# Selective scan: the diagonals of B for one of three pairs of states, made by VectorE in one product per block instead of ScalarE in four activations

## The chip, the cores and the metric

The kernel is written for Trainium2 and runs on one core of one chip. Times are device microseconds (us) of the whole program. Three timed runs gave a median of 30857.69 us (30847.12 to 30858.35). Beside them stands one profiled execution, from which every duration below comes.

## The reference

Four layers follow each other on an image tensor of 4 x 64 x 64 x 192: x = x + layer(group_norm(x)). Layer 0, 1 and 3 are selective scans, Layer 2 is a Toeplitz mixer. The change concerns Layer 3 alone, whose core is:

```python
proj = jnp.einsum('kbcl,kcd->kbld', xs, x_proj_w)          # four ways k of reading the image
Bm, Cm = proj[..., dr:dr + N], proj[..., dr + N:]          # N = 16 states
delta = jax.nn.softplus(...)                               # per position and channel
def step(state, inp):
    d, b, c, uu = inp
    dA = jnp.exp(d[..., None] * A_neg[:, None, :, :])
    state = dA * state + (d * uu)[..., None] * b[:, :, None, :]
    y = jnp.einsum('kbcn,kbn->kbc', state, c)
    return (state, y)
```

There are 192 channels, 16 states and 4096 positions for each of four ways and each of four images. The part that matters here is the input of the recurrence, `(d * uu) * b`: for each state n, the value delta*u of a channel and position times B of that state at that position.

## The kernel before

**Tiling.** Layer 3 takes one image after the other (`ss2d`). For each, `ss2d_input` makes the normalized and convolved u, `ss2d_scan` scans it, `ss2d_output` sums up and projects. A scan is cut into 32 jobs: four ways (two forward, two reversed, in the order forward, reversed, forward, reversed) times eight chunks of 512 positions. A job has three groups of 64 channels. A tile of 128 partitions holds 64 channels twice, for two halves of the states; with two states along the free axis, one tile of 128x1024 holds a group and a pair index p (0 to 3), that is four states. So a job has 12 units (group, p). Their order is written out by hand in `TWO` and `ONE`; in this text they are numbered in that order: unit 0 (p 0), 1 (p 0), 2 (p 3), 3 (p 1), 4 (p 1), 5 (p 3), 6 (p 2), 7 (p 2) for the first two groups, then 8 (p 0), 9 (p 3), 10 (p 1), 11 (p 2) for the third.

**A unit.** `feed` makes `b`, the input of the recurrence, two units ahead (`AHEAD`), and `dA`, two exponentials of ScalarE (line 401). `scan` runs the recurrence on VectorE, two instructions of 128x512 (line 418, `h`), with `dA` in SBUF and `b` in PSUM; then GpSimd multiplies by C (line 422, `hc`, 128x1024). `collect` sums over the states on TensorE (line 447, `y`). A carry copy on ScalarE (line 428) saves the last state for the next chunk.

**How b is made.** For p 0, 1 and 2 TensorE makes `b` out of `dtuT`, which is delta*u with positions on the partitions, times a diagonal matrix that holds B of one state over 128 positions (line 378). These diagonals, `diag`, are made in `fetch`: for each of four blocks of 128 positions (`part`, `NB` = 4) and each of four states one activation on ScalarE, identity times a column of `bt` (line 332). That is 48 activations of 128x128 in a job. For p 3 (`direct`) GpSimd multiplies instead (line 351, `bs`), so GpSimd has 12 `hc` and 3 `bs` in a job.

**Other work of a job.** `project` and `turn_b` make `xd` and `bt`; `step_size` and `finish` make delta (ScalarE, with a softplus and its two table loads) and `dtu` (VectorE, line 278, both inputs in SBUF); `turn` transposes it. At the end of each of two channel parts, `add` writes the result: in forward ways ScalarE copies `y`, in reversed ways VectorE adds the earlier way's result (line 614, `out`). The second part has 64 rows and goes through a fold on TensorE first (`fold_ps`, line 625).

**What sets the order.** `plan` gives each load and each block of a diagonal a step: a diagonal for p is due `LEAD_DIAG` = 10 steps ahead of its first use, one block per step. There are six buffers of `diag`, four of `h`, five of `hc`, three of `dA` and two of `b`. The program is then built by a scheduler that sets the order of instructions on each engine; each engine works through its own order, with waits on the others.

Of the kernel before, what the change touches and what calls it, by code (L numbers as in the profile page):

```python
# [36 lines left out]
class Kernel:  # L37
# [270 lines left out]
    def fetch(self, job, name, key, pools, part):  # L308


        nc = self.nc
        if name in ("both", "dtu2") and job["carry"] is not None:
            one = job[name][key] = pools[name].tile([128, T], F32, name=name)
            of, P, ch = job["delta" if name == "both" else "dtu"], job["P"], key * 64
            while ch < key * 64 + 64:
                t, row = divmod(ch, P)
                rows = min(P - row, key * 64 + 64 - ch)
                for q in range(2):
                    to = q * 64 + ch % 64
                    nc.sync.dma_start(one[to : to + rows, :], of[row : row + rows, t, :])  # L320
                ch += rows
        elif name in ("both", "dtu2"):
            one = job[name][key] = pools[name].tile([128, T], F32, name=name)
            src = job["deltas" if name == "both" else "dtus"][key * 64 : (key + 1) * 64, :]
            for q in range(2):
                nc.sync.dma_start(one[q * 64 : (q + 1) * 64, :], src)
        elif name == "diag":
            if part == 0:
                job["diag"][key] = pools["diag"].tile([128, NB, 4, 128], F32, name="diag")
            for n in range(4):  # L330
                to, of = job["diag"][key][:, part, n, :], job["bt"][:, part, 4 * key + n : 4 * key + n + 1]
                nc.scalar.activation(to, self.ident, AF.Copy, scale=of)  # L332
        else:
            one = pools[name].tile([128, 2 * T], F32, name=name)
            job["cbc" if name == "c" else "bbc"][key] = one
            for q in range(2):
                row = N + 8 * q + 2 * key if name == "c" else 4 * key + 2 * q
                src = job["bc"][row : row + 2, :].rearrange("a l -> (a l)")
                nc.sync.dma_start(one[q * 64 : (q + 1) * 64, :], src.unsqueeze(0).broadcast_to([64, 2 * T]))
# [216 lines left out]
    def ss2d_scan(self, pre, u_d, y_d, P, NT, ways, A, dtb):  # L556
        tc, nc, ins = self.tc, self.nc, self.i
        DI = P * NT
        bufs = dict(c=5, bc=2, diag=5, both=6, dtu2=2) if NT == 3 else dict(c=6, bc=2, diag=6, both=6, dtu2=4)
        with (  # L560
            tc.tile_pool(name="s_w", bufs=2) as pw,
            tc.tile_pool(name="s_prep", bufs=2) as prep,
            tc.tile_pool(name="s_work", bufs=2) as work,
            tc.tile_pool(name="s_c", bufs=bufs["c"]) as cp,
            tc.tile_pool(name="s_bc", bufs=bufs["bc"]) as bcp,
            tc.tile_pool(name="s_diag", bufs=bufs["diag"]) as dp,
            tc.tile_pool(name="s_both", bufs=bufs["both"]) as both,
            tc.tile_pool(name="s_dtu2", bufs=bufs["dtu2"]) as dtu2,
            tc.tile_pool(name="s_mm", bufs=2, space=PSUM) as mm,
            tc.tile_pool(name="s_b", bufs=2, space=PSUM) as bp,  # L570
            tc.tile_pool(name="s_y", bufs=2, space=PSUM) as yp,
        ):
            pools = {"prep": prep, "work": work, "c": cp, "diag": dp, "both": both, "mm": mm, "b": bp, "y": yp,
                     "bc": bcp, "dtu2": dtu2, "bufs": bufs, "behind": 3, "lag": 0}
            jobs = []
            carry = {
                (g, p): pw.tile([128, 2], F32, name=f"carry{g}_{p}", bufs=1)
                for g in range(DI // 64) for p in range(PAIRS)
            }
            when = {  # L580
                3: dict(load=-33, project=-29, turn_b=-27, step_size=(-21, -19, -17), finish=-15,
                        turn=(-12, -10, -8), direct={3: (1,)}),
                2: dict(load=-25, project=-21, turn_b=-19, step_size=(-17, -16), finish=-14,
                        turn=(-9, -8), direct={3: (0, 1)}),
            }[NT]
            direct = when["direct"]

            for k, (col, rev) in sorted(enumerate(ways), key=lambda one: one[1]):
                w = {"dtb": dtb[:, k, :], "A": A[:, k]}

                def weights(k=k, w=w):

                    w["xw"] = self.load(pw, "xw", ins[f"{pre}x_w"][k])
                    w["dtw"] = self.load(pw, "dtw", ins[f"{pre}dt_w"][k])

                for c in range(NCH - 1, -1, -1) if rev else range(NCH):
                    first = not jobs or jobs[-1]["k"] != k
                    job = {"before": {}}
                    s = slice(c * T, (c + 1) * T)

                    def load(job=job, col=col, s=s):
                        job["u"] = self.load(prep, "u", u_d[col][:, :, s])

                    def earlier(t, job=job, col=col, s=s):
                        rows = y_d[col][t * 128 : min(DI, t * 128 + 128), s]
                        job["before"][t] = self.load(work, "earlier", rows)

                    def add(t, job=job, col=col, rev=rev, s=s):
                        y, rows = job["y"][t], min(128, DI - t * 128)

                        def last(y=y):
                            out = work.tile([rows, T], F32, name="out", bufs=3)
                            if rev:
                                nc.vector.tensor_add(out, y, job["before"].pop(t))
                            else:
                                nc.scalar.copy(out, y)
                            nc.scalar.dma_start(y_d[col][t * 128 : t * 128 + rows, s], out)

                        def halves():
                            both = work.tile([128, T], F32, name="out", bufs=3)  # L620
                            nc.scalar.copy(both, y)

                            def sum_them():
                                one = mm.tile([64, T], F32, name="fold_ps", tag="mm")
                                nc.tensor.matmul(one, self.fold, both, start=True, stop=True)
                                return lambda: last(one)

                            return sum_them

                        return halves if rows == 64 else last  # L630

                    steps = [(when["load"], load)]
                    if first:
                        steps.append((when["load"] + (0 if len(jobs) == 0 else -2), weights))
                    if rev:
                        for t in range(-(-DI // 128)):
                            steps.append((8 * t + 2, lambda t=t, earlier=earlier: earlier(t)))
                    job.update(
                        P=P, NT=NT, DI=DI, k=k, w=w, rev=rev, carry=carry, first=first, add=add, y={}, fed={},
                        done={}, bs={}, when=when, steps=steps, direct=direct,  # L640
                    )
                    jobs.append(job)
            self.run_jobs(jobs, pools)
# [586 lines left out]
```

## Time and profile before

| what | value |
|---|---|
| median of three runs | 30857.69 us |
| profiled execution, its own time | 30865.86 us |
| its span | 30864.0 us |
| TensorE, VectorE, ScalarE, GpSimd busy in the span | 26878.4, 22327.6, 23000.6, 22890.6 us |
| activations that make diagonals, all layers | 20480, mean 391 ns |
| of these in Layer 3 | 6144 |
| `hc` in Layer 3 on GpSimd | 1536, median 2367 ns |
| Layer 3's scans | between about 24850 and 30720 us of the span |

The profile lists busy times by engine, groups of instructions with their count, busy time and mean duration, and what ended an engine's idle time. The mean duration of short instructions is longer than the distance at which they follow each other, because records overlap. A record also counts as busy when the instruction stands still behind another engine's use of the same resource. As the layers have different limits, the engine totals of the span say little about Layer 3.

### The profile page before, as it was taken

To read this page: it belongs to the slowest core of one execution; us is meant where nothing else is said; L and a number is where in the kernel's file an instruction comes from. 1 tells how busy PE (TensorE), PEld (TensorE's weight loads), DVE (VectorE), ACT (ScalarE), POOL (GpSimd) and SP (SyncE) were. 2 spreads that over 40 slices of the span, in tenths; PEclk is the share of its full clock that TensorE was granted. 3 is DMA by queue.
4 is the path that set the end of the run, shared out by engine and by line. 5 is a ranking of instruction groups with operands and counts; after the bars stand their busy time and mean duration, and the time that the engine had idled before them with its cause. 6 is when DMAs were issued, how large, how long until landed. Compare 5 with 4: busy or idle time off the path is not lost. (4 is left out here: it accounts for less than half of the span.)

```text
span 30864.0 us, 503255 instructions
## 1 busy us (share of the span) xinstructions
PE 26878.4 (87%) x189464; PEld 15827.7 (51%) x189464; DVE 22327.6 (72%) x16587; ACT 23000.6 (75%) x50177; POOL 22890.6 (74%) x9831
## 2 busy tenths in 40 slices
PE   8998998999899688888888888888588988888888
PEld 5664665666466444444444444444355444444444
DVE  7887888788788777777777777777423267777777
ACT  7885886788588588888888888888232278788888
POOL 7885885888588499989998999999100077777777
PEclk9999999999999899999999999999788999999999
DMA  3334333433433533333333333333533345545454
GB/s 109 100 99 117 101 98 104 112 100 99 119 101 97 142 99 97 97 100 101 101 104 97 98 97 99 102 101 102 131 78 76 104 131 131 132 130 134 128 135 128
DMA packets 1652695, 3342.38 MB, mean 108 GB/s; under 512 B 396725, under 2 KB 453494, under 8 KB 1634646
## 3 DMA queue, kind: packets, MB, share of 16 engines
q1 hardware_dynamic: 1541718, 3142.34, 38.1%
q10 hardware_dynamic: 108544, 167.85, 1.6%
q8 instruction: 1497, 24.53, 0.4%
q14 instruction: 936, 7.67, 0.1%
HBM read 2149.81 MB, written 656.08 MB: 91 GB/s over the span
## 5 line engine op out<-in xcount | busy, mean ns | idle before, releaser
L378 PE MATMUL b<-diag,dtuT 128*64 128x256 f32 x98304 | 12607.9, 386 | 1732.9 <-DVE h L411 917.9
L422 POOL TENSOR_TENSOR hc<-h,c 128x1024 f32<-128x1024 f32 x4608 | 10943.4, 2395 | 1515.0 <-DVE h L418 1158.3
L378 PEld LDWEIGHTS b<-diag,dtuT 128*64 128x64 f32 x98304 | 8214.9, 138 | 6212.3 <-DVE h L411 1903.3
L401 ACT ACTIVATE dA<-both,A 128x512 f32<-128x512 f32 (+1 forms) x12288 | 8267.7, 711 | 2124.3 <-DVE h L411 1472.0
L418 DVE TENSOR_TENSOR_SCAN h<-dA,carry,b 128x512 f32<-128x512 f32 x6720 | 8169.8, 1263 | 1367.8 <-PE b L378 861.4
L422 POOL TENSOR_TENSOR h<-h,c 128x1024 f32<-128x1024 f32 x3072 | 7219.1, 2374 | 1049.2 <-DVE h L411 880.3
L332 ACT ACTIVATE diag<-ident,bt 128x128 f32<-128x128 f32 x20480 | 6570.6, 391 | 92.2 <-issue 91.4
L447 PE MATMUL y<-hc,fold 128*64 128x512 f32 x18432 | 5783.3, 599 | 386.1 <-POOL hc L422 384.4
L411 DVE TENSOR_TENSOR_SCAN h<-dA,b 128x1024 f32<-128x1024 f32 x2304 | 5202.8, 2274 | 1147.3 <-ACT dA L401 798.4
L351 POOL TENSOR_TENSOR bs<-dtu,bc 128x1024 f32<-128x1024 f32 x1536 | 3639.4, 2369 | 158.5 <-DMA c<-bc_dram 72.8
L447 PE MATMUL y<-h,fold 128*64 128x512 f32 x12288 | 3259.6, 593 | 10.2 <-POOL h L422 10.2
L501 POOL MEMSET pad<- 128x13068 f32 (+1 forms) x8 | 73.4, 9172 | 3968.3 <-DMA inw<-in_L_in_w 2997.7
L411 DVE TENSOR_TENSOR_SCAN h<-b,bs 128x1024 f32<-128x1024 f32 x768 | 1758.9, 2290 | 1413.6 <-ACT b L401 1102.8
L447 PEld LDWEIGHTS y<-hc,fold 128*64 128x64 f32 x18432 | 1924.0, 138 | 1550.1 <-POOL hc L422 813.1
L401 ACT ACTIVATE b<-both,A 128x504 f32<-128x504 f32 (+1 forms) x3072 | 2076.2, 676 | 376.4 <-DVE h L418 328.3
L418 DVE TENSOR_TENSOR_SCAN h<-b,carry,bs 128x512 f32<-128x512 f32 x1344 | 1639.2, 1260 | 220.9 <-issue 170.4
L237 PEld LDWEIGHTS dtu_ps<-ident,dtu 128*64 128x64 f32 (+1 forms) x16384 | 1183.2, 141 | 497.6 <-issue 375.9
L447 PEld LDWEIGHTS y<-h,fold 128*64 128x64 f32 x12288 | 1005.0, 137 | 795.2 <-issue 444.9
L418 DVE TENSOR_TENSOR_SCAN h<-dA,b 128x512 f32<-128x512 f32 x960 | 1112.8, 1205 | 352.8 <-PE b L378 191.3
L401 ACT ACT_TABLE_LOAD x1019 | 1307.4, 1283 | 11.8
L237 PE MATMUL dtu_ps<-ident,dtu 128*64 128x128 f32 (+1 forms) x16384 | 1272.7, 273 | 45.9 <-DVE dtu L278 41.5
L827 DVE SCALAR_TENSOR_TENSOR u<-in_ps,conv_w,u 128x504 f32<-128x504 f32 (+2 forms) x1152 | 831.6, 722 | 411.7 <-ACT u L822 402.6
(157 smaller groups left out, 24601.4 us busy)
## 6 DMA issues: line engine op xcount, KB each, us to landing
c<-bc_dram SPq DMA_DIRECT2D x3072, 256.0 KB, 4.1
both<-delta SPq DMA_DIRECT2D x2048, 128.0 KB, 2.7
bc<-bc_dram SPq DMA_DIRECT2D x768, 256.0 KB, 4.2
both<-delta_dram SPq DMA_DIRECT2D x1536, 128.0 KB, 3.7
dtu<-dtu_dram SPq DMA_DIRECT2D x1536, 128.0 KB, 2.7
dtu<-dtu SPq DMA_DIRECT2D x1280, 128.0 KB, 2.5
L_y<-out ACTq DMA_DIRECT2D x512, 256.0 KB, 3.0
u<-L_u SPq DMA_DIRECT2D x160, 768.0 KB, 5.4
```

Of the source, the lines that this page charges most:

```text
L237: nc.tensor.matmul(to[half * 64 : (half + 1) * 64], of[:, half * 64 : (half + 1) * 64], self.ident[:p, :p], start=True, stop=True,)
L332: nc.scalar.activation(to, self.ident, AF.Copy, scale=of)
L351: self.nc.gpsimd.tensor_mul(by(b), dtu, by(job["bbc"][p]))
L378: nc.tensor.matmul(to, dtu, job["diag"][p][:, k, 2 * q : 2 * q + 2, :], start=True, stop=True,)
L401: nc.scalar.activation(to[n], of, AF.Exp, scale=w["A"][:, g, 2 * p + n : 2 * p + n + 1])
L411: nc.vector.tensor_tensor_scan(h[:, way], dA[:, way], b[:, way], 0.0, ALU.mult, ALU.add)
L418: nc.vector.tensor_tensor_scan(hn[:, n, way], dA[:, n, way], by_n[:, n, way], start, ALU.mult, ALU.add)
L422: nc.gpsimd.tensor_mul(hc, h, job["cbc"][p])
L447: nc.tensor.matmul(y[c * 64 : (c + 1) * 64, :], self.fold, of, start=first == 0 and n == 0, stop=last == LAST and n == 1)
L501: nc.gpsimd.memset(pad, 0.0)
L827: nc.vector.scalar_tensor_tensor(u[:, :, to], ps[:, :, of], tap(3 - j), u[:, :, to], ALU.mult, ALU.add)
```

## The change

For p = 2 in Layer 3 the four activations of a block are replaced by one VectorE instruction of 128x512. It multiplies the identity, repeated four times, by four columns of `bt`, each repeated along 128 elements. Layer 0 has an empty list, and Layer 1 has none; their diagonals stay with ScalarE.

```diff
         elif name == "diag":
             if part == 0:
                 job["diag"][key] = pools["diag"].tile([128, NB, 4, 128], F32, name="diag")
+            if key in job.get("whole", ()):
+                by_n = job["bt"][:, part, 4 * key : 4 * key + 4].unsqueeze(2).broadcast_to([128, 4, 128])
+                whole = self.ident.unsqueeze(1).broadcast_to([128, 4, 128])
+                nc.vector.tensor_mul(job["diag"][key][:, part], whole, by_n)
+                return
             for n in range(4):
                 to, of = job["diag"][key][:, part, n, :], job["bt"][:, part, 4 * key + n : 4 * key + n + 1]
                 nc.scalar.activation(to, self.ident, AF.Copy, scale=of)
...
-                        turn=(-12, -10, -8), direct={3: (1,)}),
+                        turn=(-12, -10, -8), direct={3: (1,)}, whole=()),
...
-                        turn=(-9, -8), direct={3: (0, 1)}),
+                        turn=(-9, -8), direct={3: (0, 1)}, whole=(2,)),
...
-                        done={}, bs={}, when=when, steps=steps, direct=direct,
+                        done={}, bs={}, when=when, steps=steps, direct=direct, whole=when["whole"],
```

## The prediction

> **What bounds the kernel now.** I read the page first (engine totals, slices), then looked only at the stretches of Layer 3's scan, because the change touches nothing else. On the page ScalarE and GpSimd are both busy 74 to 75% of the whole span, which decides nothing. The table of windows over single jobs does:
>
> ```profile
> core 0: us, PE busy (x) PEld busy (x) DVE busy (x) ACT busy (x) POOL busy (x), PEclk, DMA share, GB/s
> 28168.70:28208.00 39.30, 34.23 (x255) 20.00 (x253) 30.89 (x25) 37.56 (x96) 35.38 (x16) 1.00 0.53 137
> 28398.30:28435.50 37.20, 33.20 (x262) 20.38 (x260) 31.26 (x27) 36.59 (x95) 36.08 (x16) 1.00 0.56 148
> ```
>
> The first window is one job of a forward way, the second one of a reversed way. The copy that begins a job (`xd<-xd_ps`) recurs every 39.32 us in forward ways and every 37.16 us in reversed ones. ScalarE leaves 1.7 us and 0.6 us of that free: it is the bound. GpSimd is next, with 35.4 to 36.1 us. So a gain can't be larger than the distance to GpSimd. ScalarE's groups over the forward job:
>
> ```profile
> L332 ACT ACTIVATE diag<-ident,bt 128x128 f32<-128x128 f32 x47 | 15.1, 391 | 0.0
> L401 ACT ACTIVATE dA<-both,A 128x512 f32<-128x512 f32 x18 | 11.9, 709 | 1.2 <-issue 1.2
> ```
>
> 15.1 us for 47 is 0.32 us each (the mean of 391 ns overlaps its neighbours). The waits over 28080 to 28640 show how the engines are tied:
>
> ```profile
> PEld y L447 <- POOL hc L422: 78.2, 58, 2.3
> ...
> POOL hc L422 <- DVE h L418: 28.9, 42, 2.4
> ...
> DVE out L614 <- PE y L447: 17.7, 8, 2.5
> ```
>
> Columns: total us, times, longest. TensorE waits for GpSimd, GpSimd for VectorE, and VectorE's `out` for TensorE: a ring in which one late step comes round again.
>
> One VectorE instruction of today has what the new one will have, two inputs in SBUF beside a busy GpSimd: `dtu`. By source line over Layer 3, and in the timeline of a forward job:
>
> ```profile
> L278 DVE TENSOR_TENSOR dtu<-delta,u x128: 1194/1839/3002, 24861.3 to 30642.7; 96x1024 f32<-96x1024 f32 x128
> ```
>
> ```profile
> 28148.55 5.63 POOL L422 TENSOR_TENSOR hc<-h,c 128x1024 f32<-128x1024 f32 x2
> ...
> 28150.11 1.86 DVE L278 TENSOR_TENSOR dtu<-delta,u 96x1024 f32<-96x1024 f32 x1 [0.75 <-ACT delta L271]
> ```
>
> Min, median and max are 1194, 1839 and 3002 ns for one shape. The pair of `hc` takes 5.63 us, where a pair not beside a `dtu` takes 4.7. VectorE waited for GpSimd's running product and then held off the next one for 0.95 us.
>
> **What the Trainium skill says.** "SBUF — State Buffer", section "Who interferes with whom": a VectorE instruction with two SBUF inputs contends with a GpSimd instruction that reads SBUF, as an exclusive lock over the whole instruction; the loser waits. The trace agrees (the `dtu` above; my reading of its 128 cases: 1.08 us of work after GpSimd's product ends). "VectorE: DVE Perf Modes", section "The perf-mode tier table": an fp32 `tensor_tensor` has no faster mode, 2293 ns for 2048 elements, so about 0.6 us for 512, an estimate. The trace agrees: a 96x512 instruction with two SBUF inputs (`acc`, line 664) takes 739 ns, 0.65 start to start. What happens when VectorE has several such instructions in a row while GpSimd has work is seen in Layer 0's input stage:
>
> ```profile
> 111.09 25.83 DVE L545 SCALAR_TENSOR_TENSOR o<-pad,cw,o 128x4096 f32<-128x4096 f32 x4
> ```
>
> ```profile
> 122.57 15.28 POOL L536 COPY by_col<-one 128x512 f32<-128x512 f32 x3
> ```
>
> Three copies of about 1.0 us each took 15.28 us, 5.1 us apiece: each waited for most of one VectorE instruction (4.48 us when alone) and then ran, instead of the three running in 3.1 us together. The engines take turns.
>
> **The change, part by part.** Removed: 16 activations per job on ScalarE, 128 jobs: 2048 x 0.32 = 655 us of ScalarE, 5.1 us per job. ScalarE falls to about 32 us per job and no longer bounds. Added: 4 VectorE products per job, 512 in all, 0.6 us each by themselves, 2.4 us per job; VectorE goes from 31 to 33.5 us. No DMA is added or taken away, and GpSimd and SyncE get no new instruction. By the built program, GpSimd's order stays as it was. VectorE's is: unit 5's scan, **three products in a row**, unit 6's scan, the fourth product, unit 7. TensorE's order shifts too: the fold of the 64-row part, and the fill of unit 6, now stand behind the collection of unit 3's `hc` (before: behind unit 1's), and in reversed jobs `out` of the first part stands ahead of unit 9's scan on VectorE (before: behind it).
>
> Unavoidable cost on GpSimd: 15 products at 2.32 start to start = 34.8, plus 0.95 for `dtu`, 35.75 us; a 512-element product works half of `dtu`'s 1.08, 0.54, and as 1.08 costs GpSimd 0.95, 0.13 less, it costs 0.42. All four: 37.4. That alone would be 1.9 below a forward job and 0.3 above a reversed one.
>
> But the products also wait, and behind a waiting product stands unit 6's scan on VectorE; for that scan wait GpSimd's next `hc`, TensorE's fill of unit 8 and ScalarE's carry copy. I laid a job out by hand with the trace's durations (scan pair 2.35, GpSimd starts 0.25 after a scan, fill of `b` 1.95 plus 0.3, TensorE 1.8 to 2.25 from `hc` of unit 7 through the `dt_ps` block), from the end of unit 3's `hc`.
>
> Reversed: fold and its `out` end at 2.2, unit 5's scan at 4.5; GpSimd, done with unit 4 at 2.3, waits. First product 4.5 to 5.05; `hc` 5 to 7.4; second product; `bs` to 10.2; third to 10.75; unit 6's scan to 13.05, fourth product to 13.6. GpSimd has nothing from 10.2 to 13.6. `hc` 6 and 7 end at 15.9 and 18.5, TensorE is through at 20.8, `out` to 21.6, unit 9's scan to 24.0, and GpSimd, done with `hc` 8 at 20.8, waits until 24.2. The remaining units follow with unit 3's `hc` ending at 46.1. Check by GpSimd: work 34.8 + 0.95 + 0.4, idle 2.7 + 3.4 + 3.4 + small gaps 0.4 = 46.1. That is +8.9 against 37.16.
>
> Forward: no `out` on VectorE. Unit 5's scan, held by `bs` 5, ends 0.9 after unit 3's `hc`, when `hc` 4 runs: first product waits to 2.3, second behind `hc` 5 (5.65), third behind `bs` 9 (8.45); scan and fourth product to 11.35, GpSimd idle 7.9 to 11.35; later 1.0 us behind the softplus and its table loads. Unit 3 again at 41.5: +2.2 against 39.32.
>
> Sum: per image 16 reversed jobs and 14 forward ones (two more are the start-up): 4 x (16 x 8.9 + 14 x 2.2) = 693 us. The profiled execution has 30865.86 us (span 30864.0, 1.9 us around it), 8.2 above the median of the runs, 30857.69. So 31550.
>
> Bounds: the trace has no 512-element product of this kind beside GpSimd. A product costs at least its 0.6 us and, where it meets GpSimd, up to a whole product more, 2.9; I take the full wait where the layout meets a running product. The shift of TensorE's order could by itself cost nothing (fills that are early anyway) or even gain; I take what the layout gives, since `out` waited up to 2.5 us for `y` before. Costed at nothing are the carry copies, the `both`, `c` and `bc` loads on SyncE (they run two units or more ahead, and the cycle gets longer, not shorter) and the start-up. If the loads' lead is gone, one late `c` costs 3 us once, as the waits show for one.
>
> **Rivals.** *One wait for the three products.* If they run together (or broadcast inputs need no lock), only the first waits or none. The layout then gives about 43.5 and 38.8: 4 x (16 x 6.3 - 14 x 0.5) = 375 us, 31230. For it: the three stand directly behind one another in VectorE's order, and the second needs nothing that is late. Against: the three copies of Layer 0, which got in between VectorE's instructions one by one.
>
> *VectorE's lead absorbs the waits* (the other side). `h` has four buffers, so VectorE may be three units, 7 us, ahead of GpSimd; if that holds through the products, GpSimd never starves and a job is its 37.4 in both ways: 4 x (16 x 0.3 - 14 x 1.9) = -87 us, 30770. It decides below a mean of about 38.2 per job. For it: ScalarE's lateness, which keeps VectorE close behind today, goes. Against: the waits show GpSimd waiting for VectorE in reversed jobs already, and TensorE's fills stand behind collections, so that the lead can't grow while GpSimd is behind.
>
> *The change doesn't do what it says:* excluded by the built program, which has 512 products and 2048 activations less.
>
> **How the numbers follow.** Turns as laid out: 0.6 (31300 to 31800). One wait: 0.2 (31000 to 31300). Partial loss, 30920 to 31000: 0.05. No change within 0.2% (62 us, about what a measurement of this kernel can tell): 0.06. Lead absorbs: 0.09. So faster 0.09, same 0.06, slower 0.85. The range 30940 to 31800 leaves out both last cases at the low end and some 0.04 above.
>
> **What would show it.** Right: `diag` on VectorE with a median near or above 2 us and a minimum of 0.6; jobs of more than 39.3 us in both ways; GpSimd's idle time behind `h` larger, and VectorE's `out` behind `y`; ScalarE near 32 us per job. Wrong: reversed jobs at 37 to 38, or a median of `diag` near 0.7.

## The result, and the profile after

The changed kernel takes 31615.09 us (median of 4 runs, 31605.55 to 31636.58). The kernel before, run beside it, takes 30858.02 us (4 runs, 30847.12 to 30867.71). The ratio is 1.0246, with a 95% interval of 1.0229 to 1.0264: 757 us slower. The profiled execution has 31605.55 us and a span of 31603.7 us.

The table of windows over one forward and one reversed job of the last image but one answers to the first lines that the prediction showed. Columns are the stretch, its length, and busy time (number) of each engine.

```profile
core 0: us, PE busy (x) PEld busy (x) DVE busy (x) ACT busy (x) POOL busy (x), PEclk, DMA share, GB/s
28531.00:28575.20 44.20, 36.10 (x263) 21.90 (x262) 40.04 (x31) 33.25 (x80) 37.22 (x15) 0.96 0.44 116
29499.50:29544.20 44.70, 36.52 (x262) 22.03 (x260) 33.45 (x32) 32.65 (x79) 37.95 (x15) 0.96 0.46 123
```

ScalarE is down by about 4 us and no longer bounds. But no other engine fills the job either. VectorE's 40.04 us of the forward job contain products that stand still behind GpSimd (below), and GpSimd, next in line, now stands idle for 7 us of each job, where it had 3.9 and 1.1 us before. So the job isn't longer because an engine has more work than fits, but because the engines wait for each other. By the copy that begins a job, forward jobs take 44.2 us (39.3 before) and reversed ones 44.7 us (37.2 before). TensorE's granted clock (PEclk) is 0.96 in these jobs, where it was 1.00 before; what that can mean is taken up behind the experiments.

The groups of the forward job, by form:

```profile
L427 POOL TENSOR_TENSOR hc<-h,c 128x1024 f32<-128x1024 f32 x12 | 29.9, 2505 | 6.9 <-DVE h L423 3.9 <-PE b L383 3.0
...
L337 ACT ACTIVATE diag<-ident,bt 128x128 f32<-128x128 f32 x32 | 10.4, 392 | 0.5 <-issue 0.5
L333 DVE TENSOR_TENSOR diag<-ident,bt 128x512 f32<-128x512 f32 x4 | 8.3, 2123 | 0.0
```

The activations of the diagonals went from 47 to 32 and from 15.1 to 10.4 us. The four new products show 8.3 us here, though each works 0.65 us. The idle 6.9 us ahead of `hc` is all of GpSimd's: it waits for a recurrence, or for the fill that the recurrence waits for.

The waits over the whole of Layer 3, before and after (total us, times, longest; PEld is TensorE's weight load):

```profile
PEld y L447 <- POOL hc L422: 778.8, 557, 3.9
...
POOL hc L422 <- DVE h L418: 426.1, 363, 34.9
PE y L447 <- POOL hc L422: 366.0, 361, 3.4
...
DVE h L418 <- ACT dA L401: 243.6, 207, 4.1
...
DVE h L418 <- PE b L378: 167.4, 206, 8.8
...
DVE out L614 <- PE y L447: 149.2, 60, 6.7
...
ACT xd L217 <- PE xd_ps L209: 116.1, 70, 14.3
```

```profile
PEld y L452 <- POOL hc L427: 1325.3, 710, 4.4
PE y L452 <- POOL hc L427: 850.1, 508, 3.5
POOL hc L427 <- DVE h L423: 772.4, 358, 34.1
...
ACT xd L217 <- PE xd_ps L209: 377.2, 123, 14.1
...
DVE h L423 <- PE b L383: 314.9, 214, 6.7
...
DVE out L619 <- PE y L452: 275.8, 60, 6.7
...
DVE out L619 <- PE fold_ps L630: 204.6, 60, 7.0
...
DVE h L423 <- ACT dA L406: 37.6, 31, 5.8
```

TensorE's wait for GpSimd nearly doubles (778.8 + 366.0 to 1325.3 + 850.1), and so does GpSimd's for VectorE; these waits lie beside each other and are not to be added up. VectorE's `out` waits 480 us in all, 205 of them for the fold (before: 177, 28 of them for the fold). Its recurrences `h` wait longer for the fills, 314.9 us instead of 167.4, and far less for ScalarE's `dA`, 37.6 us instead of 243.6. ScalarE's `xd` waits for TensorE 377.2 us in 123 jobs (before: 116.1 us in 70). This last wait wasn't in the prediction.

The products themselves, by tile over Layer 3 (min, median, max in ns; the count at the end of such a line is only that of the records looked at for their shape):

```profile
L333 DVE TENSOR_TENSOR diag<-ident,bt x512: 654/677/2860, 24866.6 to 31400.8; 128x512 f32<-128x512 f32 x171
```

Most of them take 0.68 us, and only where they meet GpSimd up to 2.9. In the timeline both kinds are seen. First VectorE and then GpSimd in a forward job (start, us, operation, count):

```profile
28566.37 7.68 DVE L333 TENSOR_TENSOR diag<-ident,bt 128x512 f32<-128x512 f32 x3
```

```profile
28563.31 7.44 POOL L427 TENSOR_TENSOR hc<-h,c 128x1024 f32<-128x1024 f32 x3
28570.70 2.80 POOL L356 TENSOR_TENSOR bs<-dtu,bc 128x1024 f32<-128x1024 f32 x1
```

and in a reversed job:

```profile
29500.50 1.86 DVE L333 TENSOR_TENSOR diag<-ident,bt 128x512 f32<-128x512 f32 x3
```

```profile
29500.75 3.84 POOL L427 TENSOR_TENSOR hc<-h,c 128x1024 f32<-128x1024 f32 x1 [2.92 <-DVE h L423]
29504.56 2.99 POOL L356 TENSOR_TENSOR bs<-dtu,bc 128x1024 f32<-128x1024 f32 x1
```

In the forward job the engines take turns: three products need 7.68 us. In the reversed job the three run in 1.86 us, one behind the other, and GpSimd's `hc`, on record from 0.25 us after the first began, is held until the last is through: 3.84 us instead of 2.35. The two jobs differ in what GpSimd does when the first product starts: in the forward job it is in the middle of an `hc`, in the reversed one it has stood idle for 2.92 us and begins after it. All 128 jobs of the trace divide nearly the same way. In the 64 in which a GpSimd instruction was running, GpSimd got in between the products each time. In the 64 in which none was, the three ran in a row in 60. The traces of experiments 3 and 8 below say the same: GpSimd got in 101 of 101 and 124 of 124 times where it was running, and 3 of 27 and 0 of 4 times where it was not.

### The profile page after: what moved, and what is told of

It is laid out like the page before. It is cut to its first block, busy times and chain, and to the rows that moved or that the text cites. A ratio compares the mean times of both kernels' runs of the same rounds, so it can differ in the third digit from the quotient of the medians.

```text
span 31603.7 us, 501827 instructions
## 1 busy us (share of the span) xinstructions
PE 27149.9 (86%) x189464; PEld 15998.5 (51%) x189464; DVE 22999.1 (73%) x17099; ACT 22469.5 (71%) x48129; POOL 23086.4 (73%) x9831
## 4 chain that ended last, share of the span: by engine, by line
PE 31%; ACT 25%; DVE 16%; POOL 14%; issue 7%; DMA 5%; SPq 1%; ACTq 0%; POOLq 0%; DVEq 0%
PE b L383 12%; ACT diag L337 8%; DVE h L423 7%; ACT dA L406 6%; POOL h L427 6%; PE y L452 6%; DVE h L416 4%; POOL hc L427 4%; POOL bs L356 4%; ACT L406 2%; ACT b L406 2%; PE yt_ps L1085 2%; PE conv_ps L538 2%; DMA xn<-t_xn 2%; PE dtu_ps L237 1%
## 5 line engine op out<-in xcount | busy, mean ns | idle before, releaser
L427 POOL TENSOR_TENSOR hc<-h,c 128x1024 f32<-128x1024 f32 x4608 | 11072.0, 2425 | 2050.5 <-DVE h L423 1520.4
L383 PEld LDWEIGHTS b<-diag,dtuT 128*64 128x64 f32 x98304 | 8323.7, 138 | 6113.0 <-DVE h L416 1905.0
L337 ACT ACTIVATE diag<-ident,bt 128x128 f32<-128x128 f32 x18432 | 5914.5, 390 | 114.1 <-issue 113.4
L356 POOL TENSOR_TENSOR bs<-dtu,bc 128x1024 f32<-128x1024 f32 x1536 | 3708.3, 2414 | 158.0 <-DMA c<-bc_dram 72.5
L237 PEld LDWEIGHTS dtu_ps<-ident,dtu 128*64 128x64 f32 (+1 forms) x16384 | 1252.5, 145 | 546.5 <-issue 420.6
L237 PE MATMUL dtu_ps<-ident,dtu 128*64 128x128 f32 (+1 forms) x16384 | 1361.9, 279 | 45.9 <-DVE dtu L278 41.5
```

Source lines behind the costliest of these rows:

```text
L237: nc.tensor.matmul(to[half * 64 : (half + 1) * 64], of[:, half * 64 : (half + 1) * 64], self.ident[:p, :p], start=True, stop=True,)
L356: self.nc.gpsimd.tensor_mul(by(b), dtu, by(job["bbc"][p]))
L383: nc.tensor.matmul(to, dtu, job["diag"][p][:, k, 2 * q : 2 * q + 2, :], start=True, stop=True,)
L427: nc.gpsimd.tensor_mul(hc, h, job["cbc"][p])
```

## The experiments

Each number is the median of runs on one chip, beside the kernel before on the same chip. Four chips were used (experiments 1 to 4, 5 to 8, 9 and 10, 11 and 12); the kernel before had 30865 to 30871 us on them and 30858 beside the change, so that differences between chips carry some us. Job lengths are means over Layer 3, without the first and the last job of each eight of one way; so counted, the kernel before has 39.4 us forward and 37.2 reversed, and the changed kernel 44.2 and 44.9. The "shared read interface" of the expectations is the contention that the prediction describes, of a VectorE instruction with two SBUF inputs and a GpSimd instruction.

Two orders matter for what follows. In both, `y n` is the collection of unit n, `b n` a fill; the end of one reversed job and the start of the next, on TensorE as built (a fill that is split is shown once):

```
before:  b3 b4 y1 y0 y1 fold_ps dtu_ps        b6 | xd_ps  y2 y3 b7 dtu_ps y2 y3 b_ps b8
after:   b3 y1 y0 b4 y1 y2 y3 y2 fold_ps dtu_ps b6 | xd_ps  b7 y3 y4 dtu_ps       b_ps b8
```

After the change the fold, the fill of unit 6 and `xd_ps` all stand behind collections of units 2 and 3, and so behind GpSimd's `hc` of unit 3. On VectorE, `out` of the first part stands behind unit 9's scan before the change and behind unit 8's after it, as the prediction says.

**1. No products, and no activations either.** In the kernel before, the diagonals of p 2 are left out (its fills read those of p 1). The scheduler then gives TensorE the order of the changed kernel, and puts `out` on VectorE where the changed kernel has it.

```diff
         elif name == "diag":
+            if job["P"] < 128 and key == 2:
+                job["diag"][key] = job["diag"][1]
+                return
```

> The kernel before, with the diagonals for p 2 left out altogether (the fills of p 2 read those of p 1 instead): neither ScalarE's 16 activations per job nor VectorE's 4 products. The built program has TensorE's and VectorE's order of the changed kernel (fold and fill of unit 6 behind the collection of hc 3; out ahead of unit 9). Theory 'products' (the waits of and for the four VectorE products, by the shared read interface, cost the time): without products GpSimd keeps going; by my layout 41.6 us per reversed and about 37 per forward job, some 31010 us. Theory 'order' (the order of TensorE, which shifted because ScalarE became lighter, costs the time): within 1% of the changed kernel, 31300 to 31700 us, jobs of 43 to 45 us though there is less work than in either kernel.

Measured: 31491.45 us (31487.79 to 31511.41), ratio 1.0205 [1.0188, 1.0222]; jobs of 44.1 us forward and 43.5 us reversed, inside the 'order' expectation. VectorE has no added instruction, ScalarE has 16 fewer per job, and 627 of the 757 us are still lost. Its waits over Layer 3 look like those of the changed kernel:

```profile
PEld y L450 <- POOL hc L425: 1253.4, 638, 4.4
...
POOL hc L425 <- DVE h L421: 924.6, 357, 33.4
PE y L450 <- POOL hc L425: 834.8, 457, 3.5
...
ACT xd L217 <- PE xd_ps L209: 372.1, 121, 13.0
...
DVE h L421 <- ACT dA L404: 328.9, 141, 4.8
```

So the products' turns with GpSimd are not what made most of the loss. What is left in common is the order. One wait differs: here the recurrences do wait for `dA`, 328.9 us.

**2. The changed kernel with its products spread**, one behind each of units 6, 7, 8 and 9 instead of three in a row (a pin keeps an instruction, on its engine, behind what the program text has before it):

```diff
-                nc.vector.tensor_mul(job["diag"][key][:, part], whole, by_n)
+                one = nc.vector.tensor_mul(job["diag"][key][:, part], whole, by_n)
+                self.tc.keep_in_program_order(one)
```

> The changed kernel with each of the four products pinned behind the scan that is traced before it, so that one product stands behind each of units 6, 7, 8 and 9 instead of three in a row behind unit 5. TensorE's order is that of the changed kernel. Theory 'products': the turns with GpSimd are no longer one behind another; 1 to 3 us less per job, 31250 to 31500 us. Theory 'order': no real change, 31550 to 31700 us.

Measured: 31643.26 us (31632.39 to 31647.96), ratio 1.0252 [1.0237, 1.0267]; the changed kernel has 1.0246. That the products stood in a row was not the cause there: this is the 'order' expectation again.

**3. The changed kernel with the order kept**: the collections on TensorE and the reversed ways' `out` on VectorE are pinned in the same way. TensorE then has nearly its order of before; the products stay three behind unit 5 and one behind unit 6. `out` of the first part doesn't go back to its old place: it stands behind unit 11's scan, in this and the other kept runs but 7, where it is behind unit 10's.

```diff
-            nc.tensor.matmul(
+            one = nc.tensor.matmul(
...
+            if job["NT"] == 2:
+                self.tc.keep_in_program_order(one)
...
-                                nc.vector.tensor_add(out, y, job["before"].pop(t))
+                                one = nc.vector.tensor_add(out, y, job["before"].pop(t))
+                                if NT == 2:
+                                    self.tc.keep_in_program_order(one)
```

> The changed kernel, products three in a row as they are, but each collection matmul (y) and the reversed jobs' out are pinned behind what is traced before them on their engine. TensorE's fills then come ahead of the collections (fold and fill of unit 6 behind hc 1, as before the change; fills 10 and 11 ahead of the collection of units 6 and 7). Theory 'products': the products' waits remain, 40 us per job or more, at least 31150 us. Theory 'order': the loss goes, below 30900 us.

Measured: 31201.94 us (31192.52 to 31206.39), ratio 1.0109 [1.0094, 1.0124]; 41.5 and 40.6 us. 413 us come back with the order, 337 remain. The number lies within the 'products' expectation (at least 31150), but with the 413 us neither reading alone is enough. Here the turns show in the median:

```profile
L333 DVE TENSOR_TENSOR diag<-ident,bt x512: 656/2040/2936, 24868.0 to 30994.0; 128x512 f32<-128x512 f32 x171
```

**4. The order kept and the diagonals of p 2 left out**, the edits of 1 and 3 together.

> The same pins, and the diagonals for p 2 left out as in e1_no_p2 (p 1's are read): what ScalarE's relief is worth if neither products nor the shifted order stand in the way. Both theories: bounded by GpSimd's 35.75 us per job plus small gaps, 36 to 37 us in both ways, about 30600 to 30750 us. The difference of e3_kept_vector to this run is the price of the products in an unshifted order: by theory 'products' 3 us or more per job (over 350 us), by theory 'order' under 2 us per job (under 240 us).

Measured: 30749.75 us (30740.22 to 30755.28), ratio 0.9963 [0.9948, 0.9978]; 37.7 us in both ways. The time is inside the expected range; the jobs are not (36 to 37 us). In the kept order the four products, three of them in a row, cost 31201.94 - 30749.75 = 452 us, while in the shifted order they cost 31615.09 - 31491.45 = 124 us. In the shifted order GpSimd waits for recurrences even without products, 924.6 us in experiment 1 against 351.7 here; that the products fall into this idle time is argued, not shown.

**5. The order kept and the products spread**, the edits of 2 and 3 together.

> e3_kept_vector with the four products pinned one behind each of units 6, 7, 8 and 9; TensorE's order is the kept one, as in e3_kept_vector and e4_kept_no_p2. Theory 'a row of turns' (three products behind one another each wait for a GpSimd product, so the price is a matter of the row): most of e3's 452 us over e4 goes, 30800 to 30950 us. Theory 'VectorE has no room' (31 us of work plus 2.4 plus waits for b, so any place costs the same): as e3, 31100 to 31250 us.

Measured: 30972.95 us (30963.28 to 30979.34), ratio 1.0034 [1.0022, 1.0047]; 39.4 and 38.7 us. Spreading brings 229 us here. It comes near the 'row' expectation (30800 to 30950) and misses it by 23 us, because the products still cost 223 us.

**6. A stand-in without the second input.** As 4, with a reduction 128x4 <- 128x512 at each of the places of 5. It works about as long but has one input in SBUF, writes 128x4 instead of 128x512, and its result is not used.

```diff
+                by_n = job["bt"][:, part, 8:12].unsqueeze(2).broadcast_to([128, 4, 128])
+                few = pools["prep"].tile([128, 4], F32, name="few")
+                one = nc.vector.tensor_reduce(few, by_n, mybir.AxisListType.X, ALU.add)
+                self.tc.keep_in_program_order(one)
```

> e4_kept_no_p2 with a stand-in at the places of e5: a VectorE reduction over 512 elements of the same broadcast columns of bt, one SBUF input, result not used (p 2's fills read p 1's diagonals). About 0.6 us, as the product. Theory 'shared read interface': without a second SBUF input neither engine holds the other up; the stand-in has a flat duration and the time is within 100 us of e4 (30750), while e5 is above it by 100 us or more. Theory 'VectorE's time alone': e6 equals e5 within 40 us.

Measured: 30824.22 us (20 runs, 30802.58 to 30837.29), ratio 0.9986 [0.9979, 0.9992]. By tile, experiment 5 and then this one:

```profile
L333 DVE TENSOR_TENSOR diag<-ident,bt x512: 653/666/7414, 24880.1 to 30773.2; 128x512 f32<-128x512 f32 x171
```

```profile
L332 DVE TENSOR_REDUCE few<-bt x512: 647/660/672, 24909.6 to 30640.4; 128x4 f32<-128x512 f32 x171
```

Both have nearly the same median, but the reductions never take longer than 0.672 us, and the products do: 162 of the 512 took over 0.9 us, 161 of them up to 2.85 and one 7.4. The plain occupation of VectorE at these places costs 74 us, and what the product has beyond it 149 us. That this is the second input, and not the larger output, is argued here; experiment 11 speaks for it. It isn't that something waits for the products: in the traces of the change and of 2, 3, 5 and 8, no engine's wait was ended by one.

**7. The kernel before with the order kept**: the pins of 3, with all diagonals on ScalarE.

> The kernel before, all diagonals on ScalarE, with the same pins as e3 to e6. Separates the pinned order from ScalarE's relief: e4 minus this run is the relief alone. If the relief is what gains, this run is 30850 to 30950 us and e4 is 100 to 200 us below it; if the pinned order is what gains, this run is near e4's 30750.

Measured: 30872.03 us (12 runs), ratio 1.0002 [0.9993, 1.001]. Jobs take 39.5 and 37.5 us. The pins cost nothing by themselves, and ScalarE's relief is worth 30872.03 - 30749.75 = 122 us, if nothing is paid for it (with the small shift of `out` named in 3). By the job lengths it comes from the forward jobs alone: 39.5 to 37.7 us, against 37.5 and 37.7 in reversed ones.

**8. A single pin.** The changed kernel with only the collections of units 2 and 3 pinned behind the fill of unit 6.

```diff
+            if job["NT"] == 2 and t == 0 and first == 3:
+                self.tc.keep_in_program_order(one)
```

> The changed kernel, products three in a row, with one thing pinned: the collections of units 2 and 3 stay behind the fill of unit 6 on TensorE. In the built program the fold and fills 6 and 7 then no longer stand behind hc 3 (and out stands behind unit 10's scan). If that one place in TensorE's order carries the loss, this run is at e3's 31200 or below; if the other shifts (fill 10 behind the collection of unit 7) matter as well, 31350 to 31600.

Measured: 31390.79 us (31387.4 to 31396.12), ratio 1.017 [1.0154, 1.0185]. With this pin the scheduler also moved `out` of the first part, from behind unit 8's scan to behind unit 10's. Together they bring 224 of the 413 us; the rest lies in the other shifts, which were not separated.

**9 and 10. One tile in SBUF, in narrow instructions.** The order kept, and the identity times one column of `bt` as a scalar, 16 instructions of 128x128 per job (9, shown), or 8 with the other two blocks left on ScalarE (10).

```diff
-            if key in job.get("whole", ()):
...
             for n in range(4):
                 to, of = job["diag"][key][:, part, n, :], job["bt"][:, part, 4 * key + n : 4 * key + n + 1]
-                nc.scalar.activation(to, self.ident, AF.Copy, scale=of)
+                if key in job.get("whole", ()):
+                    one = nc.vector.tensor_scalar_mul(to, self.ident, of)
+                    self.tc.keep_in_program_order(one)
+                else:
+                    nc.scalar.activation(to, self.ident, AF.Copy, scale=of)
```

> All of p 2's diagonals stay on VectorE, but as 16 tensor_scalar instructions of 128x128 per job (the identity times one column of bt as a scalar), four behind each of units 6 to 9, with TensorE and 'out' in the kept order. Only one input is then a tile in SBUF. Theory 'second SBUF input': they run without turns with GpSimd at 0.15 to 0.2 us each, 2.4 to 3.2 us per job, so about what the stand-in reduction cost: 30800 to 30870 us, between 100 and 170 under the kept, spread products (30973). Rival 'any VectorE instruction on SBUF pays': like the kept, spread products or above, 30950 to 31050.

> As the run before, but only blocks 1 and 3 of p 2 go to VectorE (8 tensor_scalar instructions per job, four behind unit 7 and four behind unit 9); blocks 0 and 2 stay with ScalarE. If ScalarE is the bound only by the 0.9 us per job that its whole relief brought (122 us), half the relief brings most of that, and VectorE pays half: 30780 to 30830 us. Rival: relief counts in proportion, and so does the price, so that it lies half way between the kept kernel with ScalarE alone (30872) and the run before.

Measured: 32216.76 us (32215.27 to 32224.08), ratio 1.0436 [1.0422, 1.045], and 31508.6 us (31497.66 to 31517.44), ratio 1.0206 [1.0192, 1.022]. The first reading missed by far in both. So did the rival of 9, which had 31050 us at most. The rival of 10, half way between 30872 us and experiment 9, that is 31544 us, came within 36 us: relief and price count nearly in proportion. By tile, and in VectorE's and GpSimd's timelines of experiment 9:

```profile
L333 DVE TENSOR_SCALAR diag<-ident,bt x2048: 250/275/2422, 24888.8 to 32025.1; 128x128 f32<-128x128 f32 x187
```

```profile
30005.00 5.06 DVE L333 TENSOR_SCALAR diag<-ident,bt 128x128 f32<-128x128 f32 x4
```

```profile
30005.25 2.43 POOL L426 TENSOR_TENSOR hc<-h,c 128x1024 f32<-128x1024 f32 x1 [2.82 <-DVE h L422]
30007.62 2.35 POOL L355 TENSOR_TENSOR bs<-dtu,bc 128x1024 f32<-128x1024 f32 x1
```

Four instructions that take 0.25 us each when alone need 5.06 us: two run, then GpSimd's `hc`, then the third, then `bs`, then the fourth. With one tile input this instruction meets GpSimd just as the product does. The Trainium skill says so, and my expectation had left it out: "SBUF — State Buffer", section "Who interferes with whom", names beside two SBUF inputs a VectorE instruction in a mode that reads through both ports, and counts `tensor_scalar` among those that can enter one; "VectorE: DVE Perf Modes", section "The perf-mode tier table", gives `tensor_scalar` a faster mode (2x) in fp32 and `tensor_reduce` none. The waits agree on both: up to 2.422 us here, never over 0.680 for the reductions (experiments 6 and 12). The mode itself isn't seen in a trace, and the column of `bt` lies in SBUF as well; no run separates the two.

**11. B read from PSUM.** The order kept, and products of 128x512 as in the change, but made at `turn_b`, four in a row, straight from the transposes' result, so that only the identity lies in SBUF. They have three buffers of their own, and the other diagonals four instead of six.

```diff
+            def after():
+                evacuate(bt.rearrange("p (h k) n -> p k h n", h=2), of)
+                for key in job.get("whole", ()):
+                    to = job["diag"][key] = prep.tile([128, NB, 4, 128], F32, name="diag_whole", bufs=3)
...
+                        by_n = of[:, part % 2, part // 2, 4 * key : 4 * key + 4].unsqueeze(2).broadcast_to([128, 4, 128])
+                        one = nc.vector.tensor_mul(to[:, part], whole, by_n)
...
```

> p 2's diagonals on VectorE, in the kept order of TensorE, but each 128x512 product reads B straight from the transposes' result in PSUM (b_ps), so that only the identity is an input in SBUF. The four stand in a row at turn_b, between the two recurrences of unit 8; each diagonal lives longer, in three buffers of its own (four instead of six for p 0 and 1). Theory 'second SBUF input': about 0.65 us each without turns, the price of the stand-in reductions: 30780 to 30870 us, under the kernel before. Rival 'a product pays whatever it reads, or four in a row pay': 30950 us or more, with durations above 0.7 us in the median.

Measured: 30846.15 us (13 runs, 30824.64 to 30865.88) beside 30870.83 us (18 runs, 30857.01 to 30882.94), ratio 0.9992 [0.9983, 1.0]. By tile:

```profile
L259 DVE TENSOR_TENSOR diag_whole<-ident,b_ps x512: 660/680/689, 24848.4 to 30597.1; 128x512 f32<-128x512 f32 x171
```

No product waits any more (max 0.689), though GpSimd was busy beside 409 of the 512. The trace shows one new wait: TensorE's `dt_ps`, which takes turns with the transposes' result in the same two PSUM buffers, waited 62.7 us in 45 cases until a product had read it. With the order kept, this makes the same diagonals at 769 us less than the change. Against the kernel before it is a gain of 25 us, whose interval reaches to no gain at all.

**12. Stand-ins in a row.** As 6, with three of the reductions in a row behind unit 6 and one behind unit 7.

> Kept order, p 2's diagonals left out (its fills read those of p 1), and four stand-in reductions of 128x512 with one input in SBUF per job, three of them in a row behind unit 6 and one behind unit 7. The step of 229 us from spread products to three in a row had two readings. If the turns with GpSimd make it, a row without turns costs what the spread stand-ins cost: 30800 to 30860 us. If the delay of 2 us that a row puts ahead of the next recurrence makes it, about 31000 us.

Measured: 30757.35 us (30744.53 to 30763.3), ratio 0.9962 [0.9949, 0.9975]: 8 us above leaving all out, and below both expectations. A row of 2 us on VectorE ahead of a recurrence is no cost by itself at this place, one unit later than the products of experiment 3. So by this stand-in 445 of the 452 us of experiment 3 are the turns, as far as the one unit and the unused result don't matter.

## Why the prediction came out as it did

The sum of 693 us stands against 757 measured, and the sign was right. Its parts were not, and that they add up so well is luck.

- **The two causes.** By the same layout without products (expectation of experiment 1, written after the result: some 31010 us) the order alone makes about 150 of the 693 us, and the products with their turns the other 540. Measured, the shifted order without products loses 627 us, and the products add 124. One term is some 470 us too small and the other some 420 too large.
- **The shift of TensorE's order** is the term that was mis-sized. The prediction wrote that it "could by itself cost nothing (fills that are early anyway) or even gain". The layout had followed the fold and the fill of unit 6 to behind unit 3's `hc`, but not `xd_ps`, which stands behind the same collections: ScalarE's `xd` waits 377.2 us instead of 116.1. How this delay reaches the recurrences isn't shown. In the changed kernel they wait less for `dA` than before (37.6 us against 243.6), and more for the fills (314.9 against 167.4); VectorE's `out` waits more as well (480 against 177). Forward jobs were put at 41.5 and take 44.2.
- **The turns** held in 52 of 64 forward jobs; in the one shown the three products take 7.68 us, much as laid out. In 48 of 64 reversed ones they run in a row, 1.86 us in the one shown, which was the rival "one wait for the three products". So the median is 677 ns, and the prediction had named a median near 0.7 as a sign that it was wrong: for this step it was. Reversed jobs were put at 46.1 and take 44.7.
- **The price of one product**, 0.6 us alone and up to 2.9 beside GpSimd, is 0.654 and 2.860 us.
- **ScalarE's relief** was put at 5.1 us per job and is 4.3 in the forward job shown and 3.9 in the reversed one. It doesn't reach the bound that the prediction names, GpSimd's work: that is 35.75 us by its count where no product waits, and with the order kept and nothing paid, jobs still take 37.7 us (experiment 4).
- **The total by ways** shows the same luck: forward jobs are 2.7 us longer than forecast and reversed ones 1.4 shorter, 4 x (14 x 2.7 - 16 x 1.4) = 62 us, against the 65 us by which 31615 exceeds 31550.
- **The rival of the other side**, that VectorE's lead absorbs the waits (30770), is near the 30757 us of experiment 12 in its number, but there none of the added instructions waits for GpSimd. Where the products of the change do wait, with the order kept, 452 us are lost: the lead does not absorb them.

By the runs, the 757 us are built up like this:

| step | from | us |
|---|---|---|
| pins alone | exp. 7 less before | +4 |
| ScalarE relieved of 16 activations per job | 4 less 7 | -122 |
| VectorE busy four times 0.66 us, spread | 6 less 4 | +74 |
| second input in SBUF, spread | 5 less 6 | +149 |
| three in a row instead of spread | 3 less 5 | +229 |
| order no longer kept | after less 3 | +413 |

These add up to 747, which is the changed kernel less the 30867.78 us that the kernel before had beside experiments 5 to 8; beside the change it had 30858.02. The steps are not independent, and the table is one way through them: with the order shifted, the products cost only 124 us, and with it kept 452; the order costs 413 us with the products, and 31491.45 - 30749.75 = 742 without them.

**TensorE's clock** is a rival that no run was made for. In the stretch from 25100 to 25900 us, inside the first scan, the granted clock is 1.00 in the kernel before, 0.95 in the changed one, 0.96 in experiment 1, 0.93 in 3, 0.98 in 4 and 0.96 in 7. It doesn't order the runs: experiment 7 has 0.96 and the time of before, and experiment 3 has less clock than the changed kernel and takes 413 us less. What share it has in single steps stays open.

**Left open.** By what rule a waiting engine comes next: what GpSimd does when the first product starts tells the jobs apart, but why it then gets in, or doesn't, at every later product isn't shown. By which waits the shifted order lengthens a job. Why stand-ins spread over four units cost 74 us and in a row 8. And why products out of PSUM (30846) cost 89 us more than the stand-ins in a row; they also differ in their place and in the buffers, and `dt_ps` waits for them. That the lighter ScalarE is what moves the scheduler is argued from experiment 1, where besides only the diagonals that the fills of p 2 read are others; the scheduler's own reasons were not looked into.

## What to carry to other kernels

Where a scheduler sets the order, an edit is also a change of everything that the scheduler then puts elsewhere: do the edit with the order held, and the order's shift with the edit left out, before its own price is blamed or praised. When an instruction moves behind a wait, follow every other one that now stands behind the same wait, and then read from the waits which engine really stands still for it. Before work is moved to VectorE beside a busy GpSimd, look at what it reads: its duration says little. Here 2048 instructions of 0.25 us cost 1467 us in the kept order, 512 of 0.66 us at the same places 223, and the same products from PSUM didn't wait at all.

## What the runs showed of the hardware

- A 128x128 `tensor_scalar` with one tile in SBUF waited for GpSimd's running product, up to 2.42 us for 0.25 us of work; 2048 of them cost 1467 us in the kept order (experiment 9 less 4).
- VectorE instructions of 0.65 us that reduce one tile in SBUF (experiments 6 and 12) ran beside a busy GpSimd in all 512 cases each and never took over 0.68 us. Those that read one tile in SBUF and one in PSUM (experiment 11) met a busy GpSimd in 409 of 512 cases and never took over 0.69 us.
- Three two-input products behind one another let GpSimd in between whenever one of its instructions was running as the first of them started (64 of 64 jobs of the change, 101 of 101 and 124 of 124 in experiments 3 and 8). Where none was, they mostly held GpSimd off until all three were through (60 of 64, 24 of 27, 4 of 4).
